# First stage traced in source order, the weight generator run in pairs, first weights requested on a second queue

## The chip, the core and the metric

The kernel runs on one core of a Trainium2 chip. The metric is the device time of one execution in microseconds (us); lower is better. A core has TensorE (PE: matrix products into PSUM, with a separate record, PEld, for loading the stationary operand), VectorE (DVE), ScalarE (ACT), GpSimd (POOL) and SyncE (SP, which here only issues DMAs). [...] The profile is one execution; its lines L12 are lines of the kernel before.

## What is computed

Four layers follow each other on x of 64 sequences, 64 tokens, 256 features, with a condition vector of 64 numbers for each sequence. The first layer, which the change is about, in the reference:

```python
scale = cond @ norm_w.T + 1.0
ms = jnp.mean(x * x, axis=-1, keepdims=True)
h = x * (scale[:, None, :] * jax.lax.rsqrt(ms + EPS))
u = h @ up_w.T                                  # up_w: 2048 x 256
val, gate = jnp.split(u, 2, axis=-1)
h = val * jax.nn.gelu(gate, approximate=False)
hq = act_quant(h)                               # round(h * 127 / max|h|), per token
wq = weight_quant(down_w)                       # -1, 0 or 1
y = hq @ wq.T + x
```

Then come attention with conditioned norms, a gated feed-forward layer with conditioned norms, a layer norm with a bias from the condition, and an adapter whose two matrices are made for every sequence from its condition (`(h_lang @ Wdd.T + bdd) * 0.1`: 64 x 32768 numbers for each of the two). This making of the adapter's matrices is the "generator" below.

## The kernel before, in words

**Stages.** The 4096 tokens are eight blocks (NBLK) of 512 (T), each of four tiles (TT) of 128. Stage one is layer one (`l0`) with the generator beside it, stage two attention with first parts of the feed-forward layer, stage three the rest. Between stages data goes through DRAM (`x1d`, `x2d`, and `s1d`, `s2d` for the generator's output).

**Exact products.** A product in full precision is `mm3` (L83, L84, L85): both operands are split in a high part (a cast to fp32r on ScalarE) and a low part (a subtraction on DVE or GpSimd), and three matmuls are summed.

**Stage one.** The loop at L380 runs over visits n = 0 to 33, one for each 128-token tile and two to drain. A visit calls `upper(n, 0)` and `upper(n, 1)`: each makes gate and value for half the hidden features, two banks of six matmuls of 512 columns (12 matmuls), then GELU on ScalarE (L336) and value times GELU on DVE (L337). Between the halves stands one generator unit: `gen_make` (four fp32 products of 64 x 64 by 64 x 512, eight matmul records, into two banks, L251), `gen_load` of a later unit's 512 KB (`gt`), and, after the second half, `gen_store` (two ScalarE copies to `stg`, L261, and two DMAs issued by GpSimd, L263). `quant(n)` (L343 to L349: maximum, scale, round, clip on DVE) ends in a transposing DMA on SP (`qt`), and `lower(n - 2)` multiplies `qt` with the ternary weights (L363, eight matmuls) and adds x (L364). Every fourth visit `prep` loads the next block twice (`xf` features first, `xt` tokens first), scales and splits it (L315, L198, L199) and finds the root mean squares (L191 on ScalarE, L182 and L184 on GpSimd).

**Things done once.** `cond_norm` (L113, L120) makes layer one's scale, `load_up(j)` loads and splits a quarter of the up weights (L280, L281), `ternary` and `ternary_rest` make the -1/0/1 weights (L291, L299, L304 to L306), `cond_rest` makes the other conditioning vectors (L113, L155, copies L143, L156). Hooks at chosen visits call `cond_rest` (visit 4), `weights` (the split of attention's weights, visits 8 to 15) and, in the last visits, attention's first steps: `a_start` (load, mean squares, scale L205), `a_norm` (transposes L212, L215, L216, split) and `a_ahead` (values, queries and keys).

**What sets the order.** In stage one and three a planner orders each engine's instructions by its own costs. In stage two, from L841 to L922, `manual_schedule` fixes the order of PE, ACT, DVE and POOL to that of the source. SP's DMAs are left to the planner in all stages. Buffers are handed out per tag; PSUM's eight banks all have one tag in stage one, the 512 KB blocks share five buffers (tag `x1`).

Of the kernel before, what the change touches and what calls it, by code (L numbers as in the profile page):

```python
# [36 lines left out]
def tile_kernel(ctx: ExitStack, tc, xT, x, condT, cw, upT, downT, qkvT, woT, ghT, outT_w,  # L37
# [52 lines left out]

    ident = const.tile([P, P], F32, name="ident")
# [4 lines left out]
    for s in range(2):  # L96
        nc.sync.dma_start(out=ct[s * 64:(s + 1) * 64], in_=condT)

    gl = pools["a"].tile([P, NB], F32, name="gl")
    nc.vector.tensor_scalar(gl, ct, 0.1, None, ALU.mult)  # L100
# [9 lines left out]
    def cond_vector(cwv):  # L110
        pb = bank("mm")
        for c in range(2):
            nc.tensor.matmul(pb[:, c * NB:(c + 1) * NB], lhsT=cwv[:, c * P:(c + 1) * P], rhs=ct[0:64],  # L113
                             start=True, stop=True)
        return pb[:, 0:2 * NB].rearrange("p (c b) -> p c b", c=2)

    def cond_norm():
        cwn = main.tile([64, D], F32, tag="st", bufs=2, name="cwn")
        nc.sync.dma_start(out=cwn, in_=cw[:, V_NORM, :])
        nc.vector.tensor_scalar(cv[:, V_NORM], cond_vector(cwn), 1.0, None, ALU.add)  # L120

    def cond_rest():
# [8 lines left out]
        nc.sync.dma_start(out=vc, in_=vecs)  # L131
        nc.vector.tensor_tensor(w2, vc[:, 1, :], vc[:, 1, :], ALU.mult)
        bo = main.tile([NB, D], F32, tag="junk", bufs=1, name="bo")
        nc.sync.dma_start(out=bo, in_=rows[0:1, :].broadcast_to([NB, D]))
        al = main.tile([NB, 3, D], F32, tag="xn", bufs=1, name="al")
        for v0 in (1, 5):
            n = min(4, 8 - v0)
            cwt = main.tile([64, 4, D], F32, tag="x1", bufs=X1, name=f"cwt{v0}")
            nc.sync.dma_start(out=cwt[:, :n], in_=cw[:, v0:v0 + n, :])
            for v in range(v0, v0 + n):  # L140
                src = cond_vector(cwt[:, v - v0])
                if v != V_LIN:
                    nc.vector.tensor_copy(cv[:, v], src)  # L143
                    continue

                th = main.tile([P, 2, NB], F32, tag="st", bufs=2, name="th")
                for c in range(2):
                    nc.scalar.activation(th[:, c], src[:, c], AF.Tanh, bias=vc[:, 3, c:c + 1])
                    nc.vector.tensor_scalar(th[:, c], th[:, c], vc[:, 2, c:c + 1], vc[:, 1, c:c + 1],
                                            ALU.add, ALU.mult)  # L150
                    nc.vector.tensor_scalar(cv[:, v, c], th[:, c], vc[:, 2, c:c + 1], None, ALU.add)
            for i, v in enumerate((V_AA, V_FA)):
                if v0 <= v < v0 + n:
                    pb = bank("mm")
                    nc.tensor.matmul(pb[:NB, :D], lhsT=ct[0:64], rhs=cwt[:, v - v0], start=True, stop=True)  # L155
                    nc.vector.tensor_copy(al[:, i], pb[:NB, :D])  # L156
        nc.vector.tensor_tensor(al[:, 2], al[:, 1], bo, ALU.mult)
        nc.gpsimd.dma_start(out=alphad.rearrange("v b d -> b v d"), in_=al)


    def split_steps(hi, lo, src, kc, n, step):
        v = src.rearrange("(c p) n -> p c n", p=P)
        for c in range(kc):
            for j in range(0, n, step):
                uid[0] += 1
                st = main.tile([P, 512], F32, tag="st", bufs=2, name=f"st{uid[0]}")
                nc.sync.dma_start(out=st[:, :step], in_=v[:, c, j:j + step])
                nc.scalar.copy(hi[:, c, j:j + step], st[:, :step])
                nc.vector.tensor_tensor(lo[:, c, j:j + step], st[:, :step],
                                        hi[:, c, j:j + step].bitcast(F32), ALU.subtract)  # L170
                yield True
# [63 lines left out]
    def gen_load():  # L235
        if gen_left:
            g, sd, k = gen_left.pop(0)
            ks = slice(k * 2 * GC, (k + 1) * 2 * GC)
            uid[0] += 1
            gt = pools["a"].tile([P, 2 * GC], F32, tag="gt", bufs=3, name=f"gt{uid[0]}")  # L240
            nc.sync.dma_start(out=gt, in_=g[:, ks])
            gen_loaded.append((gt, sd.rearrange("s b x y -> b s (x y)")[:, :, ks]))
# [23 lines left out]
    def l0(hooks):  # L266
# [8 lines left out]
        def load_up(j):  # L275
            js = slice(j * 512, (j + 1) * 512)
            st = main.tile([P, 2, 512], F32, tag="x1", bufs=X1, name=f"upst{j}")
            nc.sync.dma_start(out=st, in_=upT.rearrange("(c p) n -> p c n", p=P)[:, :, js])
            for c in range(2):
                nc.scalar.copy(up[0][:, c, js], st[:, c])  # L280
                nc.vector.tensor_tensor(up[1][:, c, js], st[:, c], up[0][:, c, js].bitcast(F32), ALU.subtract)  # L281

        def ternary():
            dv = downT.rearrange("(f p) d -> p f d", p=P)
            ones = main.tile([P, P], F32, tag="junk", bufs=1, name="ones")
            nc.gpsimd.memset(ones, 1.0)
            wd = [block(f"wd{j}") for j in range(2)]
            for j in range(2):
                nc.sync.dma_start(out=wd[j], in_=dv[:, 4 * j:4 * j + 4, :])
                wj = main.tile([P, 4, D], F32, tag="xn", bufs=1, name=f"wj{j}")  # L290
                nc.scalar.activation(wj, wd[j], AF.Abs, accum_out=sa[:, j:j + 1])  # L291
# [723 lines left out]
```

## Time and profile before

| what | us |
|---|---|
| median of three runs | 807.06 (805.04 to 807.66) |
| the profiled execution | 804.37 |
| its span, first to last instruction | 802.2 |
| TensorE busy in it | 763.5 |
| stage one's products, first to last `upper` | 11.3 to 266.6 |
| a steady visit of stage one | 7.70 |
| first scores of attention | 279.3 |

The span is what the profile sees of the execution; 2.2 us lie around it. "Busy" is the time in which an engine has an instruction running; matmuls overlap in their records, so steps from start to start tell more than durations. In the lines of waits, the number in brackets is the idle time ahead of an instruction and what ended it; "issue" is a wait for nothing that the profile shows. The granted clock is given as a share of TensorE's full speed.

### The profile page before, as it was taken

Reading aid. Unit: us, or ns where it says so; the run is one execution under the profiler, and the core shown is the slowest. Engines: PE = TensorE matmul, PEld = TensorE weight load, DVE = VectorE, ACT = ScalarE, POOL = GpSimd, SP = SyncE. Lnnn points to the kernel's source line nnn. Section 1 sums busy time; section 2 is a strip of 40 time slices with the busy share of each in tenths; the row PEclk is TensorE's granted clock in tenths of the full one; section 3 lists DMA queues with packets and bytes.
Section 4 is the critical chain, followed back from the end, with each engine's and each line's share of the span. In section 5 each row is a group of like instructions: output and inputs, shape, how many; then the busy total and the mean of one; then the engine's idle time right before and its main releaser. Section 6 shows DMA issues by size and latency. Waiting matters only on the chain.

```text
span 802.2 us, 17323 instructions
## 1 busy us (share of the span) xinstructions
PE 763.5 (95%) x7014; PEld 620.2 (77%) x7014; DVE 567.2 (71%) x935; ACT 370.5 (46%) x758; POOL 325.7 (41%) x300
## 2 busy tenths in 40 slices
PE   5999999999999979999999999879999999999996
PEld 3676766667667868888887878778888888888885
DVE  4885866667667679999989875555666666665755
ACT  6524542443443558887877673223233333333130
POOL 2212221222225315545545316945454545454500
PEclk9989999999999999999999999989999999999999
DMA  8997989878884764545655129616161616160401
GB/s 296 308 252 223 233 230 241 203 221 206 190 259 106 145 158 96 131 133 133 153 139 120 40 69 236 131 28 180 35 180 39 173 44 167 50 161 28 133 1 54
DMA packets 117135, 118.87 MB, mean 148 GB/s; under 512 B 39568, under 2 KB 100624, under 8 KB 117056
## 3 DMA queue, kind: packets, MB, share of 16 engines
q1 hardware_dynamic: 109568, 92.40, 46.1%
q0 software_dynamic: 7488, 25.37, 10.4%
q8 instruction: 55, 0.90, 0.5%
q14 instruction: 24, 0.20, 0.1%
HBM read 71.41 MB, written 29.56 MB: 126 GB/s over the span
## 4 chain that ended last, share of the span: by engine, by line
PE 79%; DVE 9%; issue 4%; POOL 3%; DMA 3%; ACT 1%; SPq 0%; DVEq 0%; POOLq 0%; ACTq 0%
PE mm L83 10%; PE mm L84 10%; PE mm L85 10%; PE gh L83 7%; PE gh L85 6%; PE gh L84 6%; PE mm L251 4%; PE acc L85 4%; PE mm L363 4%; PE acc L84 4%; PE acc L83 4%; DMA x2d<-ax 2%; PE mm L520 2%; PE mm L212 2%; PE mm L713 2%
## 5 line engine op out<-in xcount | busy, mean ns | idle before, releaser
L83 PE MATMUL mm<-up,xhl 128*128 128x512 f32 x256 | 108.9, 425 | 2.2 <-ACT up L280 2.2
L84 PE MATMUL mm<-up,xhl 128*128 128x512 f32 x256 | 102.8, 402 | 0.1
L85 PE MATMUL mm<-up,xll 128*128 128x512 f32 x256 | 102.5, 401 | 0.0
L83 PE MATMUL gh<-xhf,gh 128*128 128x512 f32 x244 | 99.2, 407 | 0.0
L84 PE MATMUL gh<-xlf,gh 128*128 128x512 f32 x244 | 95.6, 392 | 0.5 <-POOL xlf L199 0.5
L85 PE MATMUL gh<-xhf,gh 128*128 128x512 f32 x244 | 95.8, 393 | 0.0
L642 ACT CAST hhi<-sg 128x512 fp32r<-128x512 f32 x61 | 37.9, 621 | 119.1 <-DVE sg L623 119.1
L337 DVE SCALAR_TENSOR_TENSOR h<-mm,rs_l,g 128x512 f32<-128x512 f32 x64 | 47.7, 745 | 59.5 <-PE mm L85 36.5
L623 DVE TENSOR_TENSOR sg<-gh,sg 128x512 f32<-128x512 f32 x61 | 41.7, 683 | 64.8 <-PE gh L85 58.2
L85 PE MATMUL acc<-wout,hlo 128*128 128x256 f32 x256 | 74.0, 289 | 7.9 <-DVE hlo L643 7.9
L83 PEld LDWEIGHTS mm<-up,xhl 128*128 128x128 f32 x256 | 49.2, 192 | 38.5 <-issue 18.7
L336 ACT ACTIVATE g<-mm,rs_l 128x512 f32<-128x512 f32 x64 | 44.0, 687 | 73.0 <-PE mm L85 66.9
L83 PE MATMUL acc<-wout,hhi 128*128 128x256 f32 x256 | 73.4, 287 | 1.6 <-ACT hhi L642 1.6
L643 DVE TENSOR_TENSOR hlo<-sg,hhi 128x512 fp32r<-128x512 f32 x61 | 54.6, 895 | 26.7 <-ACT hhi L642 26.3
L84 PE MATMUL acc<-wout,hhi 128*128 128x256 f32 x256 | 73.3, 286 | 0.0
L216 POOL TENSOR_TENSOR xg<-xg,cv 128x512 f32<-128x512 f32 x32 | 33.2, 1046 | 70.7 <-DVE xg L215 70.7
L622 ACT ACTIVATE sg<-gh 128x512 f32<-128x512 f32 x61 | 36.3, 595 | 50.6 <-PE gh L85 50.6
L261 ACT COPY stg<-mm 128x512 f32<-128x512 f32 x64 | 35.3, 587 | 50.9 <-PE mm L251 50.9
L85 PEld LDWEIGHTS mm<-up,xll 128*128 128x128 f32 x256 | 49.0, 192 | 11.9
L84 PEld LDWEIGHTS mm<-up,xhl 128*128 128x128 f32 x256 | 49.3, 193 | 9.8 <-DVE up L281 0.6
L85 PEld LDWEIGHTS acc<-wout,hlo 128*128 128x128 f32 x256 | 49.5, 193 | 8.6 <-DVE hlo L643 8.6
L85 PEld LDWEIGHTS gh<-xhf,gh 128*128 128x128 f32 x244 | 46.0, 188 | 10.7
(189 smaller groups left out, 1905.7 us busy)
## 6 DMA issues: line engine op xcount, KB each, us to landing
gt<-in_g SPq DMA_DIRECT2D x32, 512.0 KB, 4.7
rows<-alphad SPq DMA_DIRECT2D x48, 256.0 KB, 4.0
s1d<-stg POOLq DMA_DIRECT2D x32, 256.0 KB, 5.1
s2d<-stg POOLq DMA_DIRECT2D x32, 256.0 KB, 4.8
vb<-vx SPq DMA_DIRECT2D x32, 256.0 KB, 4.5
wd<-s1d SPq DMA_DIRECT2D x32, 256.0 KB, 4.5
wu<-s2d SPq DMA_DIRECT2D x32, 256.0 KB, 5.6
xf<-in_xT SPq DMA_DIRECT2D x8, 512.0 KB, 7.0
```

Of the source, the lines that this page charges most:

```text
L83: nc.tensor.matmul(out, lhsT=l[0], rhs=r[0], start=first, stop=False)
L84: nc.tensor.matmul(out, lhsT=l[0], rhs=r[1], start=False, stop=False)
L85: nc.tensor.matmul(out, lhsT=l[1], rhs=r[0], start=False, stop=last)
L216: nc.gpsimd.tensor_tensor(b3(xg), b3(xg), bc(vb, c, i), ALU.add)
L251: nc.tensor.matmul(pb[s][c * 64:(c + 1) * 64], lhsT=gl[h], rhs=gt[h, c * GC:(c + 1) * GC], start=True, stop=True, tile_position=(64 * s, 6 ...
L261: nc.scalar.copy(stg[:, s], pb[s])
L336: nc.scalar.activation(g, pg, AF.Gelu, scale=rs[:, t:t + 1])
L337: nc.vector.scalar_tensor_tensor(h[:, ch * 512:(ch + 1) * 512], pv, rs[:, t:t + 1], g, ALU.mult, ALU.mult)
L622: nc.scalar.activation(sg, pg, AF.Silu)
L623: nc.vector.tensor_tensor(sg, pv, sg, ALU.mult)
L642: nc.scalar.copy(h_hi, sg)
L643: nc.vector.tensor_tensor(h_lo, sg, h_hi.bitcast(F32), ALU.subtract)
```

## The change

- `manual_schedule` is entered at the top, so stage one's PE, ACT, DVE and POOL follow the source too; its end stays where it was.
- The generator: in even visits from 2 on, two `gen_make` after each other between the halves, then two loads and two stores; odd visits have none. The first two units are made after the first two tiles' first products. `gt` has four buffers, not three.
- The up weights: `load_up` only loads, j = 2 and 0 on ScalarE's DMA queue as the first loads, j = 3 and 1 on SP after x and two generator blocks; `split_half` splits, the second half's subtraction on GpSimd. In the start the products of `upper(0, 0)` and `upper(1, 0)` are parted from the GELU. An early GELU on two columns (`sa`) stands ahead.
- `prep` is three steps in three visits (`prep_load`, `prep_parts`, `prep_scale`); `quant` rounds in place, before `lower` and, in the last visit, before the hooks; `lower(0)` moves to visit 3.
- `cond_rest` keeps its matmuls, but its loads go out in visit 3 (`cond_load`), its products go to three banks, and DVE copies several vectors at a time. `ternary`'s loads go to attention's memory, a visit earlier.
- Splitting of weights is a class `Splitter` that loads one piece ahead. Attention's first steps are spread over visits 25 to 33; the scale of block 2 (`a_scale(2)`) moves into attention's first step.

The diff, cut to its core:

```diff
+    ordered.enter_context(tc.manual_schedule(engines={mybir.EngineType.PE, mybir.EngineType.Activation, mybir.EngineType.DVE, mybir.EngineType.Pool}))
...
+        pbs = [bank("mm") for _ in range(3)]
         for v0 in (1, 5):
...
+            for v in range(v0, min(v0 + 4, 8)):
+                cond_vector(crest[v0][:, v - v0], pbs[v0 // 5], 2 * NB * (v - v0))
...
+        nc.vector.tensor_copy(cv[:, 1:5], src[0])
+        nc.vector.tensor_copy(cv[:, 5:7], src[1][:, 0:2])
+        nc.vector.tensor_copy(al[:, 0:2], pbs[2][:NB].rearrange("b (i d) -> b i d", i=2))
...
-            gt = pools["a"].tile([P, 2 * GC], F32, tag="gt", bufs=3, name=f"gt{uid[0]}")
+            gt = pools["a"].tile([P, 2 * GC], F32, tag="gt", bufs=4, name=f"gt{uid[0]}")
...
+        def split_half(j, c):
+            js = slice(j * 512, (j + 1) * 512)
+            st = ups[j]
+            nc.scalar.copy(up[0][:, c, js], st[:, c])
+            (nc.vector if c == 0 else nc.gpsimd).tensor_tensor(up[1][:, c, js], st[:, c],
+                                                              up[0][:, c, js].bitcast(F32), ALU.subtract)
...
+        load_up(2, nc.scalar)
+        load_up(0, nc.scalar)
+        prep_load(0)
+        nc.sync.dma_start(out=ct[64:128], in_=condT)
+        for _ in range(2):
+            gen_load()
+        load_up(3, nc.sync)
+        load_up(1, nc.sync)
...
+        nc.scalar.activation(sa, nhalf[:, 0:2], AF.Gelu)
...
         cond_norm()
+        split_half(2, 0)
+        for c, _ in enumerate(prep_parts(0)):
+            split_half((2, 0)[c], 1 - c)
+        split_half(0, 1)
+        prep_scale(0)
+        upper(0, 0, "products")
+        upper(1, 0, "products")
+        nc.vector.tensor_scalar(gl, ct, 0.1, None, ALU.mult)
+        gen_make()
+        gen_make()
+        for j in (3, 1):
+            for c in range(2):
+                split_half(j, c)
+        upper(0, 0, "rest")
+        upper(1, 0, "rest")
+        gen_store()
+        gen_store()
         gen_load()
...
         for n in range(N + 2):
             if n < N:
-                if n != 1:
+                if n > 1:
                     upper(n, 0)
+                if n % 2 == 0 and n > 0:
+                    gen_make()
+                    gen_make()
+                    gen_load()
+                    gen_load()
+                    gen_store()
+                    gen_store()
+                upper(n, 1)
...
+            if n < N - 1:
+                quant(n)
+            if n == 3:
+                lower(0)
+            if n >= 3:
                 lower(n - 2)
...
+    hooks = {3: [cond_load], 4: [cond_rest], 7: [splits.load]}
...
-    hooks[last - 5] = [lambda: a_start(0)]
-    hooks[last - 3] = [lambda: a_norm(0, 0), lambda: a_norm(0, 1)]
-    hooks[last - 2] = [lambda: a_start(1)]
+    hooks[last - 7] = [lambda: a_load(0)]
+    hooks[last - 6] = [lambda: a_begin(0)]
+    hooks[last - 5] = [lambda: a_scale(0), lambda: a_load(1)]
+    hooks[last - 4] = [lambda: a_norm(0, 0), lambda: a_begin(1)]
+    hooks[last - 3] = [lambda: a_norm(0, 1)]
+    hooks[last - 2] = [lambda: a_scale(1), lambda: a_load(2)]
...
-        if tp == 0 and w > 0:
+        if tp == 0:
             if i + 2 < NBLK:
                 a_scale(i + 2)
```

## The prediction, made before the changed kernel was run

> **What bounds the kernel now.** I read the page's busy shares first, then busy time by stretches, then the time line of TensorE in single visits.
>
> ```profile
> PE 763.5 (95%) x7014; PEld 620.2 (77%) x7014; DVE 567.2 (71%) x935; ACT 370.5 (46%) x758; POOL 325.7 (41%) x300
> ```
>
> TensorE carries the kernel. The change is in the first stage and its hand-over, so I cut that part of the span into stretches (us, then busy time per engine, granted clock, DMA share, GB/s):
>
> ```profile
> 0.00:11.31 11.31, 3.07 (x12) 1.26 (x12) 2.83 (x6) 3.48 (x6) 2.57 (x9) 1.00 0.68 227
> 11.31:28.21 16.90, 16.80 (x66) 11.40 (x67) 10.88 (x23) 14.18 (x30) 5.65 (x9) 1.00 1.04 381
> 63.80:266.56 202.76, 202.76 (x1057) 139.91 (x1053) 141.01 (x271) 86.13 (x188) 55.64 (x79) 1.00 0.82 212
> 266.56:279.32 12.76, 12.10 (x81) 10.16 (x80) 8.69 (x16) 7.91 (x21) 5.46 (x6) 1.00 0.72 138
> 279.32:296.17 16.85, 12.51 (x251) 10.91 (x252) 11.05 (x11) 9.08 (x16) 3.62 (x4) 0.93 0.78 189
> ```
>
> From 63.80 to 266.56 TensorE never pauses, so there only fewer or denser TensorE instructions count. Room lies before 11.31 (first up-projection product) and around the hand-over. A third place, inside "busy", is the conditioning step `cond_rest`:
>
> ```profile
> 51.35:56.58 5.23, 5.23 (x33) 3.90 (x32) 5.23 (x13) 0.52 (x2) 0.00 (x0) 0.85 1.09 238
> 56.58:58.05 1.47, 1.47 (x8) 1.04 (x8) 1.47 (x8) 0.00 (x0) 0.00 (x0) 0.50 1.06 376
> 58.05:61.86 3.81, 3.81 (x11) 3.04 (x10) 0.94 (x3) 0.79 (x2) 0.62 (x1) 0.50 1.34 202
> 61.86:69.55 7.69, 7.69 (x42) 5.27 (x41) 4.03 (x9) 4.15 (x14) 2.42 (x4) 1.00 0.63 191
> ```
>
> It takes 5.23 us, and the clock is halved within and after it.
>
> **Part 1: two generator units together.** One unit in a steady visit (start, duration):
>
> ```profile
> 124.06 0.40 PE L85 MATMUL mm<-up,xll 128*128 128x512 f32 x1
> 124.39 1.09 PE L251 MATMUL mm<-gt,gl 64*64 64x512 f32 x8
> 125.41 0.50 PE L83 MATMUL mm<-up,xhl 128*128 128x512 f32 x1
> 125.74 0.39 PE L84 MATMUL mm<-up,xhl 128*128 128x512 f32 x1
> ```
>
> Up products follow each other every 0.233 us. Into the unit the step is 0.33 (0.10 lost), the unit itself takes 1.02 from start to start, and out of it the step is 0.33 (0.10 lost): 1.22 us. The second four of its eight matmuls start at 124.86, 0.48 after the first four, and the change back costs 0.54. A unit directly behind another should pay two such steps, some 0.92, and no change of kind: 0.30 less. In the loop there are 15 pairs: **-4.5 us**. Bounds: 0 if the second unit waits for its banks, -6 at 0.41 saved. The four banks come back through four ScalarE copies of 0.59 us (L261), 2.4 us, in front of the next GELU. The copies overlap `upper(n, 1)` (2.8 us); with eight banks taken in turn TensorE asks for the pair's banks some 5 us after it ended. Hidden, except beside other ScalarE work: in visits 10 and 14, which have a norm (2.4 us) and a weight split as well, my tally of the queues leaves 0.53 each: **+1.1**.
>
> **Part 2: the start.** Before: the first generator block lands at 6.96, x at 8.26, the two up blocks at about 9.7 and 11.09; a 512 KB block every 1.36 us. After: ScalarE asks for the up blocks at about 0.7 and 1.2, SP for x as its third load at about 2.0. [...] Were it a path of its own, x would land 4.3 us after its issue (the first generator block's row), at 6.3. [...] three blocks at 1.36 after a first at about 5.0 make 7.5. The row of landings is one queue in strict turn[...]; I take 7.5. So the gain is the generator block that no longer goes ahead.
>
> From there: xs 0.64, the cast 0.60, first product at 8.9 (before 11.31). The low parts then pace it: five casts on ScalarE to 11.3, the last subtraction on GpSimd (1.3 us, row L199 on POOL) at 12.6, so `upper(0,0)` ends at 14.3. `upper(1,0)` follows. Before, products were 0.43 apart until 17.49, 6.2 us after the first one (the clock column has no record of this start and prints 1.00); I let the clock rise at 15.9, and `upper(1,0)` ends at 17.9. The pair 2.0, two more groups of products 5.6: `upper(2,0)` starts at 25.6. Before it starts at 28.21 with one generator unit (1.0) and L299 (0.35) more done: 26.9 for the same work. **-1.3 us**, between -3 (clock earlier) and +1 (weights j=3 and 1, now behind x and two generator blocks, late: due 19.9, landed by 14.5, split by 17.8). The second GELU table load (1.28) goes; ScalarE has the room, nothing.
>
> **Part 3: conditioning.** The loads (two `cwt`, `vc`, `bo`) go out a visit earlier, the same number on SP, whose order is not fixed by the source; DVE's eight small copies become three large. TensorE keeps its 28 L113 matmuls (0.12 apart) and four L155 (0.57 per pair at full clock): 3.4 + 1.1 = 4.5 instead of 5.2: **-0.7**. The half clock outside the step cost 0.67 in `lower` (1.47 against 0.80) and nine products at 0.43 instead of 0.233: 1.76; together **-2.4 if it does not recur**. [...] The rows decide: the clock fell at full "busy"[...]. [...] I take no drop, and keep 0 to -2.4.
>
> **Part 4: order of the source.** On DVE in-order queues cost: from the end of `upper(0,1)` (22.7) stand h 0.75, quant 3.0, h 0.75, the next block's parts 2.7, quant 3.0, two h 1.5, L297 0.16: 34.6. TensorE reaches L299 at 33.3 and waits 1.4 (with semaphores **+1.6**); behind it on its queue stands `upper(3,0)`. Then six ternary operations 4.2, two quants, four h: `lower(0)`'s last operation ends near 48.0, while `upper(4,1)` wants its bank at 47.2: **+0.75**. The 0.57 wait for wq at 38.40 goes: **-0.6**. In steady pairs DVE needs some 11.3 of 15.1: hidden. `quant` in place, `ones`, `wd` in other memory: nothing on a path.
>
> **Part 5: hand-over.** The 0.67 wait before the first scores goes, as both `lower` now follow the last copy: **-0.7**. But the norm scale of block 2 (L205, four, 1.13) moves into the first attention step, where DVE is back to back from 280.56 and TensorE already waits for it (0.93 at 287.21): **+1.1**. The load weights and x1 reads moved earlier sit under full TensorE.
>
> Sum: -4.5 + 1.1 - 1.3 - 0.7 - 2.4 + 1.6 + 0.75 - 0.6 - 0.7 + 1.1 = -5.6 us. Against the profiled execution (804.37, span 802.2) 798.8; that execution was 2.7 under the median of the runs, so for the median 807.06 - 5.6 = 801.4.
>
> **Rivals.**
> - *A stall elsewhere goes too.* Stages two and three hold gaps that nothing in this stage causes:
>
> ```profile
> 294.27 0.85 PE L539 MATMUL mm<-pts,vb 128*32 128x64 f32 x20 [3.38 <-issue]
> 525.70 0.58 PE L85 MATMUL acc<-wout,hlo 128*128 128x256 f32 x1 [7.67 <-DVE hlo L643]
> ```
>
> The first is between matmuls of one line, with data there, and an instruction packet is fetched at 291.54; its place can shift with the count of instructions ahead. The second comes from the planner's order in stage three, which the diff leaves alone. One gone: 3.4 or 7.7 more, 794 to 798. For it: they are accidents of place; against: nothing touches them, and new ones can appear.
> - *Nothing is left.* The clock drops all the same (+2.4), and x lands no earlier than before (+1.3): 805.1; with the second unit as dear as the first half of the time, 807.
> - *Slower: the transposed tile comes late.* In the visits that prepare a block, DVE now has h 0.75, parts 3.3 with the wait for the cast, quant 3.0 before the transpose goes out, 7.0 after the products; TensorE wants it after `lower` 0.8, a generator visit 8.6, two groups of products 5.7: 15.1. Slack 8.1 us; the landing is 4.3 in the median, 8.2 at most. From 8 us it decides. Behind a burst of two generator loads and four stores, 2 MB at 1.36 per 512 KB, it would be 4.3 + 5.4 = 9.7, 2 us late in seven visits: +13.5, so 815. Against it: DMA share 0.82, and the burst is spread over a visit.
>
> **Chances.** A move of less than 0.3% (2.4 us) can't be told from no change here. The forecast 0.50 (own range 798 to 805), the stall elsewhere 0.17, nothing left 0.18, the slower case 0.15. Of the first about 0.48 and of the third 0.03 lie under 804.6: faster 0.68, same 0.18, slower 0.14. The range 793 to 808 takes in the first three and leaves out the slow case and the ends.
>
> **What would show it.** Right: visits in pairs of 15.1 us, L251 x16 in one piece of about 1.95; first L83 near 8.9; no row at 0.50 clock after the conditioning step; waits of about 1.5 before L299 and 0.8 before `upper(4,1)`. Wrong: pairs at 15.4 or more; L363 waiting for qt; waits for the L261 copies; a first product after 10; a wait over 2 us before L520 in the first attention step.

## The result, and the profile after

The changed kernel takes 797.47 us in the median of four runs (794.82 to 799.51); the kernel before, run beside it, 806.94 (805.04 to 807.66). The ratio is 0.9888, with a 95% interval of 0.9858 to 0.9918: 9.5 us faster, where the prediction said 5.6. The profiled execution took 794.82 us with a span of 793.0, 9.2 less than the span of before. It is the fastest of the four and has the highest granted clock, 0.994 for 0.987 to 0.989 in the other three; what those lost, no profile shows. One of planner's twenty runs below, at 813.78 us, was in a slow state of the chip and is left out of its ratio.

First the page's row of TensorE, then busy time by stretches, cut as in the prediction (us from start to end, length; then busy time and count of TensorE, of its weight loads, of DVE, ScalarE and GpSimd; granted clock, DMA share, GB/s).

```profile
PE 752.4 (95%) x7014; PEld 618.7 (78%) x7014; DVE 575.8 (73%) x926; ACT 371.3 (47%) x758; POOL 326.2 (41%) x304
```

```profile
0.00:10.69 10.69, 1.09 (x5) 0.93 (x5) 2.12 (x5) 2.78 (x5) 2.62 (x9) 1.00 0.80 270
10.69:28.19 17.50, 17.02 (x65) 11.34 (x65) 9.98 (x13) 11.26 (x25) 9.53 (x10) 1.00 1.00 349
28.19:45.62 17.43, 15.59 (x84) 10.82 (x82) 16.25 (x29) 9.42 (x22) 4.00 (x6) 1.00 0.95 243
61.43:260.80 199.37, 199.37 (x1061) 142.43 (x1060) 154.63 (x282) 88.75 (x191) 52.26 (x79) 1.00 0.83 222
260.80:273.57 12.77, 12.10 (x82) 10.28 (x80) 6.93 (x14) 7.27 (x17) 4.54 (x4) 1.00 0.80 124
```

The row says where to look: TensorE executes the same 7014 matmuls and is busy 11.1 us less. The time went out of busy time (changes of kind, half clock), not out of idle time. Stretch by stretch: the first up product comes 0.6 us sooner (10.69 for 11.31), but the 16.90 us after it became 17.50, with the same two generator units in them. A third unit, which the kernel before made ahead of 11.31 while TensorE had nothing else to do, is now left for later; so the start got worse. The stretch from `upper(2,0)` to `upper(4,0)` has 1.84 us of idle TensorE (17.43 less 15.59), where before had 0.57. From 61.43 to 260.80 there is no idle time, as before. The hand-over is what it was, 12.77 for 12.76.

Now single visits on TensorE's time line (start, duration, engine, line, operation, output <- inputs, shapes). L269 of the changed kernel is L251 of before, the generator's matmul.

```profile
127.91 0.40 PE L85 MATMUL mm<-up,xll 128*128 128x512 f32 x1
128.24 1.95 PE L269 MATMUL mm<-gt,gl 64*64 64x512 f32 x16
130.12 0.50 PE L83 MATMUL mm<-up,xhl 128*128 128x512 f32 x1
130.46 0.39 PE L84 MATMUL mm<-up,xhl 128*128 128x512 f32 x1
```

From the product ahead of the pair (127.91) to the second one behind it (130.46) are 2.55 us; two ordinary steps of 0.233 off, the pair costs 2.08. The rows of before, read in the same way (124.06 to 125.74), give 1.21 for a unit and 2.43 for two: 0.34 less. Whole visits say the same. The first products of even visits, two in a row in the changed kernel, then two before:

```profile
80.09 0.48 PE L83 MATMUL mm<-up,xhl 128*128 128x512 f32 x1
95.15 0.48 PE L83 MATMUL mm<-up,xhl 128*128 128x512 f32 x1
```

```profile
82.91 0.48 PE L83 MATMUL mm<-up,xhl 128*128 128x512 f32 x1
98.31 0.48 PE L83 MATMUL mm<-up,xhl 128*128 128x512 f32 x1
```

They stand 15.06 us apart from 80.09 to 230.66 (150.57 for ten pairs), and 15.40 before (82.91 to 236.91). That is 0.34 a pair, 5.1 us for fifteen.

**Where the 9.2 us of the span lie.** The first scores start at 273.57 for 279.32: 5.75 us came from the first stage. The first product into `acc`, the end of the attention stage, is at 464.40 for 472.81: 2.7 us more came from a stage in which the change moves little. The last stage gave 0.8.

### The profile page after: what moved, and what is told of

The parts are those of the page before. It is cut to its first block, busy times and chain, and to the rows that moved or that the text cites. A ratio compares the mean times of both kernels' runs of the same rounds, so it can differ in the third digit from the quotient of the medians.

```text
span 793.0 us, 17333 instructions
## 1 busy us (share of the span) xinstructions
PE 752.4 (95%) x7014; PEld 618.7 (78%) x7014; DVE 575.8 (73%) x926; ACT 371.3 (47%) x758; POOL 326.2 (41%) x304
## 4 chain that ended last, share of the span: by engine, by line
PE 79%; DVE 8%; DMA 4%; issue 3%; POOL 3%; ACT 1%; SPq 1%; POOLq 0%; DVEq 0%; ACTq 0%
PE mm L83 10%; PE mm L85 10%; PE mm L84 10%; PE gh L83 6%; PE gh L85 6%; PE gh L84 6%; PE mm L269 4%; PE acc L85 4%; PE mm L396 4%; PE acc L84 3%; PE acc L83 3%; PE mm L587 2%; PE mm L230 2%; PE mm L606 2%; PE mm L794 2%
## 5 line engine op out<-in xcount | busy, mean ns | idle before, releaser
L83 PE MATMUL mm<-up,xhl 128*128 128x512 f32 x256 | 106.6, 416 | 2.2 <-ACT xhl L216 2.2
L84 PE MATMUL mm<-up,xhl 128*128 128x512 f32 x256 | 102.6, 401 | 0.5 <-DVE up L304 0.5
L83 PEld LDWEIGHTS acc<-wout,hhi 128*128 128x128 f32 x256 | 49.6, 194 | 4.2 <-ACT hhi L709 1.9
```

The lines of the kernel that those rows point to most:

```text
L83: nc.tensor.matmul(out, lhsT=l[0], rhs=r[0], start=first, stop=False)
L84: nc.tensor.matmul(out, lhsT=l[0], rhs=r[1], start=False, stop=False)
```

## The experiments

Each kernel was run beside the kernel before on the same chip, so ratios are compared, not times of different rows. Theory A was from the start: the paired units carry the gain and the other parts are small. Its rivals: the order of the source carries it; the second queue does; the packed conditioning step does.

| kernel | median us (runs) | ratio to before, 95% |
|---|---|---|
| after | 797.47 (4) | 0.9888 (0.9858 to 0.9918) |
| one_queue | 795.44 (4) | 0.9892 (0.9829 to 0.9955) |
| x_first | 799.69 (10) | 0.9926 (0.9899 to 0.9953) |
| one_unit | 803.55 (20) | 0.9987 (0.9966 to 1.0008) |
| old_cond | 816.04 (4) | 1.0135 (1.0078 to 1.0193) |
| planner | 806.35 (20) | 0.9996 (0.9973 to 1.0019) |
| cond_copies | 798.17 (4) | 0.9894 (0.9863 to 0.9925) |
| warm | 795.93 (4) | 0.9864 (0.9822 to 0.9906) |
| start | 794.16 (4) | 0.9844 (0.9808 to 0.9880) |
| tidy | 799.07 (6) | 0.9899 (0.9874 to 0.9925) |
| tidy_warm | 795.00 (6) | 0.9860 (0.9838 to 0.9882) |
| tidy_bufs | 800.00 (6) | 0.9914 (0.9893 to 0.9934) |
| start_warm | 792.50 (6) | 0.9833 (0.9797 to 0.9868) |

**one_unit: the pairs undone.**

```diff
-                if n % 2 == 0 and n > 0:
-                    gen_make()
-                    gen_make()
-                    gen_load()
-                    gen_load()
-                    gen_store()
-                    gen_store()
+                if n > 1:
+                    gen_make()
+                    gen_load()
+                    gen_store()
```

> The changed kernel with one generator unit in every visit instead of two in every other. Theory A (the pair saves one change between kinds of matmul, 0.34 us): visits of 7.70 us again, 15 times 0.34, so 5.1 us slower than the changed kernel (797.5): 802.6. Rival (source order and the moved copies make the visits shorter, the pairs do not matter): visits of 7.53, same time as the changed kernel.

803.55 us: with single units all the rest of the change is worth nothing that can be told from before (0.9987, the interval reaching over 1). Two visits take 15.40 us again, and the first scores come at 280.63, 7.06 after those of the changed kernel. Of these 5.1 are the pairs. The rest goes with a longer wait at the ternary product (2.22 for 1.35), a later clock at the start (full at 20.08 for 18.42) and a half clock of 3.41 us at 57.62; on the other side, the changed kernel's waits of 0.50 at `lower(1)` and 0.67 before the first scores are not there.

**planner: the order written by hand undone in the first stage**, with the pairs and all other edits kept.

```diff
-    ordered = ExitStack()
-    ordered.enter_context(tc.manual_schedule(engines={mybir.EngineType.PE, mybir.EngineType.Activation, mybir.EngineType.DVE, mybir.EngineType.Pool}))
 
     ident = const.tile([P, P], F32, name="ident")
...
+    ordered = ExitStack()
+    ordered.enter_context(tc.manual_schedule(engines={mybir.EngineType.PE, mybir.EngineType.Activation, mybir.EngineType.DVE, mybir.EngineType.Pool}))
     late = []
```

> The changed kernel with one thing undone: the hand-written order of TensorE, ScalarE, DVE and GpSimd begins again only at the attention stage, so the planner orders the first stage. Theory A (the gain is in the instructions themselves: fewer changes of kind of matmul, and an accidental gap in stage two): pairs of visits keep some 15.1 us, the wait before L322 (1.35) and the start change by 1 to 2 us either way, so within 3 us of the changed kernel, 795 to 801. Theory B (the order of the source carries the gain, because it keeps the two units together and the copies out of the way): the planner pulls the two units apart again or sets copies ahead of the GELUs, pairs go back to 15.4 and the first scores come 5 us later: 802 or more.

806.35 us, the time of before. Theory B has the size and not the reason: the pairs stay together (one x16 row of 1.95 us, as above), and without other waits a pair of visits takes 15.06. But `lower` waits for its transposed tile, in five visits: 1.70, 2.52, 1.77, 1.07 and 2.54, together 9.6 us. One of them on the time line (in square brackets the idle time before, and what ended it):

```profile
99.61 1.05 PE L394 MATMUL mm<-wq,qt 128*128 128x256 bf16 x8 [2.52 <-DMA qt<-q]
```

The tile that this one waited for was asked for at 91.69 and landed at 99.57, 7.9 us later. In the changed kernel the same tile was asked for at 83.54, right behind its products, and landed at 86.29; its `lower` runs at 94.34. So the planner's DVE is 8.2 us later with this tile, while its turn on TensorE came only 2.7 later (97.09), and the transposes are slower (median from issue to landing 4.71, longest 10.22; 3.40 and 8.90 in the changed kernel). This is the "slower" rival of the prediction, at 9.6 us where I had 13.5 (in an execution of 810.10, slower than planner's median). In the changed kernel only `lower(1)` waits so, 0.50; as far as these two profiles show, because the order of the source keeps DVE early. Beside one_unit it shows that the two parts need each other: order without pairs 0.9987, pairs without order 0.9996, both 0.9888.

**one_queue: the second queue undone.**

```diff
-        load_up(2, nc.scalar)
-        load_up(0, nc.scalar)
+        load_up(2, nc.sync)
+        load_up(0, nc.sync)
```

> The changed kernel with the first two blocks of up weights asked for on SP, behind ct and cwn and ahead of x, as in one queue. Theory A (the second queue lets 1 MB run ahead of the small condition weights): cwn lands near 4.4 us again (it landed at 7.2 in the changed kernel), x as third big block near 9, the first up product between 9.5 and 10.7, and the whole is 0 to 1 us faster than the changed kernel's 797.5. Theory B (a second queue is a path of its own): the up weights land 1.5 us later and the start loses 1 to 2 us.

795.44 us, ratio 0.9892 for 0.9888: the second queue is worth nothing that can be measured, though four runs leave an interval 10 us wide. The conditioning weights `cwn` land at 3.69 (for 7.23 in the changed kernel), the two up blocks at 6.38 and 7.95 (5.24 and 6.79), x at 9.28 (8.44); the first product starts at 10.77 for 10.69. What is won for one load is lost for another.

**x_first and start: what bounds the start.** x_first asks for x ahead of the two up blocks, on SP's queue; start does the same and, on ScalarE and DVE, sets x's scaling and parts ahead of the weights' casts:

```diff
-        split_half(2, 0)
-        for c, _ in enumerate(prep_parts(0)):
-            split_half((2, 0)[c], 1 - c)
-        split_half(0, 1)
+        for _ in prep_parts(0):
+            pass
+        for j in (2, 0):
+            for c in range(2):
+                split_half(j, c)
```

> The changed kernel with one queue and x ahead of the up weights: ct, cwn, x, two up blocks. Theory A (the start waits for cwn, then for x; the weights have time): cwn near 4.4, x near 6.5, first product near 8.5 instead of 10.7; the third tile's first product comes about 2 us earlier than 28.19, so 795.5 in all. Theory B (the weights pace the start): the first product is earlier, but the second weight block lands near 9 and the third tile's first product moves by less than 0.7 us.

> The changed kernel with x asked for ahead of the two up-projection blocks on SyncE, and on ScalarE and DVE x's scaling and parts ahead of the weights' casts and low parts (x alone first, with those left where they were, had gained nothing). Theory A (the start is bound by the order of landings and of the two engines' queues): x at 5.9, its parts done by 8.3, the first weights at 8.5, first product at 9.2 instead of 10.7, upper(0,0) no longer waits for low parts; upper(2,0) starts about 1.5 us sooner if the clock rises as long after the first product as in the changed kernel (6.8 us): 796. Theory B (all data of the start share the transfer rate, so that the last weight block sets it): first product near 10.5, nothing gained.

x_first missed what both theories expected. x landed at 5.90, and its first product still came at 11.14, because in the order of the source DVE has the weights' low part ahead of x's scaling, and ScalarE the weights' cast, which waits for an up block. The rows of DVE and ScalarE in x_first:

```profile
8.49 0.62 ACT L303 CAST up<-upst 128x512 fp32r<-128x512 f32 x1 [6.27 <-DMA upst<-in_upT]
9.14 0.69 DVE L304 TENSOR_TENSOR up<-upst,up 128x512 fp32r<-128x512 f32 x1 [3.92 <-ACT up L303]
9.75 1.29 DVE L346 TENSOR_TENSOR xs<-xf,cv 128x512 f32<-128x512 f32 x2
```

DVE stands idle 3.92 us in front of the low part, from 5.90 on with x there. In start the queue is turned round:

```profile
6.23 1.29 DVE L346 TENSOR_TENSOR xs<-xf,cv 128x512 f32<-128x512 f32 x2 [0.93 <-DMA xf<-in_xT]
...
9.08 0.79 PE L83 MATMUL mm<-up,xhl 128*128 128x512 f32 x1 [4.11 <-ACT up L303]
```

First product at 9.08, no wait for low parts behind it, `upper(2,0)` at 24.67 for 28.19; 794.16 us, ratio 0.9844. Theory A holds in kind; that start is faster than the changed kernel is shown by the rows, not by the times, whose intervals overlap. The 3.5 us at `upper(2,0)` are 1.6 of an earlier first product, 0.5 of the wait for a low part that went, and 1.4 of the clock: it was full 4.6 us after the first product here and 7.7 in the changed kernel, and each of the 3.1 us between loses 0.46 (steps of 0.43 for 0.233). What brought it up sooner is not shown. At `upper(8,0)` 1.9 are left, since a half clock of 3.41 us begins at 54.60.

**cond_copies and old_cond: the conditioning step.** cond_copies keeps the loads where the change put them and gives each vector a bank and a copy again, as before; old_cond puts the whole old step back, its loads too.

```diff
-        pbs = [bank("mm") for _ in range(3)]
         for v0 in (1, 5):
             for v in range(v0, min(v0 + 4, 8)):
-                cond_vector(crest[v0][:, v - v0], pbs[v0 // 5], 2 * NB * (v - v0))
...
+                one = cond_vector(crest[v0][:, v - v0], bank("mm"))
+                if v != V_LIN:
+                    nc.vector.tensor_copy(cv[:, v], one)
```

> The changed kernel with its early loads, but the conditioning step as before: a bank and a copy for each vector, eight small copies for three. Theory A (packing is worth only its own 0.8 us[...]): step of 5.2 instead of 4.44 us, with or without a half clock of 3.4 or 6.8 us behind it, 798 to 801 for 797.5. Theory B (packing is what keeps the clock up): a half clock of 6.8 us in or after the step that costs 2.4 us more, over 800.

> The changed kernel with the conditioning step of before: loads at visit 4, a bank and a copy for every vector. Theory A (its products are sparse for 5 us and halve the clock): 0.8 us more in the step and a row at half clock after it that costs another 2.4 to 3, in all 3 us or more slower: 800.5 to 802. Rival ([...]the packed form does not matter): under 1.5 us slower, no row at 0.50.

cond_copies: 798.17 us, ratio 0.9894: packing cannot be told from no packing. Its step takes 6.70 us from 52.86 to 59.56, with a wait of 0.61, for 4.27; a half clock of 6.83 us begins in it, at 55.67. old_cond is some 20 us slower than the changed kernel, far past both expectations, and for another reason than the one under test: TensorE waits for the conditioning weights themselves.

```profile
64.88 3.65 PE L116 MATMUL mm<-ct,cwt 64*128 64x64 f32 x16 [12.07 <-DMA cwt<-in_cw]
...
73.25 2.15 PE L116 MATMUL mm<-ct,cwt 64*128 64x64 f32 x9 [3.69 <-DMA cwt<-in_cw]
```

With a fixed order nothing can step ahead of these matmuls, and 23.89 us of half clock (from 55.88) go with the wait. The early loads, which I had costed at nothing, are what pays for the fixed order here.

**warm and start_warm: products to bring up the clock**, into a bank that nobody reads; warm has 30 in the changed kernel, start_warm 13 in start.

```diff
+    def warm(count):
+        pw = bank("mm")
+        for _ in range(count):
+            nc.tensor.matmul(pw[:, 0:P], lhsT=ident, rhs=ident, start=True, stop=True)
...
+        warm(5)
         cond_norm()
+        warm(8)
```

> The changed kernel with 30 fp32 products of the identity with itself (128x128, into a bank that nobody reads) put on TensorE ahead of the first up-projection, 22 ahead of the first conditioning product and 8 behind it. Theory A (the clock rises a fixed stretch of work after TensorE becomes busy): the clock is full at 10.7 when the first up product starts, products come 0.233 instead of 0.43 us apart, and the seven microseconds at half clock shrink to what DVE's and GpSimd's low parts allow: upper(2,0) starts 1.5 to 3 us before 28.19, the end likewise. Theory B (the start is paced by the low parts, and the clock only looks like the limit): upper(2,0) within 0.5 us of 28.19. The count of TensorE instructions ahead of stage two shifts by 60: if the gaps that are put down to issue hang on the place in the instruction stream, they move to other matmuls.

> The kernel called start with 13 fp32 products of the identity with itself, 5 ahead of the first conditioning product and 8 behind it, into a bank that nobody reads; at half clock each took 0.43 us in the run called tidy_warm, so that they fill TensorE from 1.35 to about 8.6 and no longer hold up the first up product (there 30 of them had put it off to 13.1). Theory A (the clock rises 3.3 to 9.1 us after TensorE begins to be busy, the spread of the runs so far, so that starting 7.7 us sooner takes away most of the 4.6 us of half clock in start): 1 to 2 us less than start, ratio 0.982 to 0.983. Theory B (at full clock the low parts pace the first products, and the wait brings the half clock back): the ratio of start, 0.984, or up to 0.986.

In warm the clock is full at 4.61, but `upper(2,0)` starts at 28.23, where it did: theory B for the start. TensorE runs out of low parts, and the clock is taken back for 3.41 us at 14.85:

```profile
12.78 0.50 PE L84 MATMUL mm<-up,xhl 128*128 128x512 f32 x1 [0.35 <-POOL up L310]
...
15.02 0.79 PE L84 MATMUL mm<-up,xhl 128*128 128x512 f32 x1 [0.96 <-DVE up L310]
```

start_warm is the fastest kernel of the study: 792.50 us, ratio 0.9833 (0.9797 to 0.9868), 13 us less than before. Against start (0.9844) the intervals overlap, so the products' own worth isn't shown by the times. `upper(2,0)` is only 0.6 sooner (24.05). The larger difference lies in the attention stage: waits there that the profile puts down to "issue" are 0.52 us in all, for 3.56 in start. The same in the other two kernels with added products: 0 in warm (4.85 in the changed kernel) and 0 in tidy_warm (4.51 in tidy). The eleven kernels without added products have 1.14 (planner) to 6.36 us (before) of them, mostly at the same matmuls block after block (358, 382, 406 and 430 us in the changed kernel; 357, 382, 406, 430 in one_queue), with sizes that differ. Beside them stand the packets of a DMA queue that the page lists, 16 KB each:

```profile
q8 instruction: 55, 0.90, 0.5%
```

Each of the 52 waits of this kind in the attention stage, over all profiles, ends 1.2 to 1.7 us after such a packet has landed (at 404.35 for the changed kernel's wait that ends at 405.84). That TensorE waits there for its next instructions is my reading; no run tries it by itself, and why the added products take nearly all of these waits away stays open.

**tidy, tidy_warm and tidy_bufs: the waits that were left.** tidy is start with the ternary sum a visit earlier, and with block 2's scaling between the first stage and the first scores:

```diff
                 nc.scalar.activation(wj, til["wd"][j], AF.Abs, accum_out=sa[:, j:j + 1])
+            nc.vector.tensor_tensor(sb[:, 0:1], sa[:, 0:1], sa[:, 1:2], ALU.add)
...
-            nc.vector.tensor_tensor(sb[:, 0:1], sa[:, 0:1], sa[:, 1:2], ALU.add)
...
+    a_scale(2)
     late = []
...
-        if tp == 0:
+        if tp == 0 and w > 0:
```

> The kernel of the run called start (x asked for first, its parts ahead of the weights' casts, one queue) with two more edits. The sum of the two ternary row sums is put on DVE a visit earlier, ahead of the next block's parts, instead of behind two further products; and the scaling of block 2 is done between the first stage's last tile and the first scores, where DVE waits anyway, instead of inside the first attention step. Theory A (both waits are only late DVE instructions): the 1.4 us before the ternary product and some 0.4 to 0.8 of the 1.3 us in the first attention step go, 1.5 to 2 us in all: 792 to 793. Theory B (a wait taken away in front of full TensorE work comes back at the next late thing, here the transposed tile that lower(1) waits 0.5 us for): no more than 0.5 us gained, 794.

> The kernel called tidy with 30 fp32 products of the identity with itself ahead of the first up product, 10 ahead of the first conditioning product and 20 behind it, into a bank that nobody reads. Theory A (the clock rises 3 to 4 us after TensorE begins to be busy, and what follows runs at full clock as long as it is fed): the 4.3 us of half clock after the first product (9.1 to 13.4) go, 1.5 to 2 us: 790.5 to 791.5. Theory B (at full clock TensorE runs out of low parts, waits a microsecond as it did at 15.0 in the run called warm, and the clock is taken back): within 1 us of tidy.

> The kernel called tidy with two buffers instead of four for the adapter's weights of the last stage, down and up, so that the planner can no longer bring the next block's four wide bias additions ahead of the normalization's inverse root on GpSimd. It bears on the 7.8 us wait of TensorE near 515, which the change left as it was. Theory A (the wait is those four additions, 9.4 us on GpSimd's queue): the wait and the half clock in it, 3.4 to 6.8 us, go: 7.8 plus 1.5 to 3 us less, some 782 to 785. Theory B (the inverse root is late for another reason, or the planner puts other work in that place; weights that are loaded later come late themselves): less than 3 us gained, or slower.

799.07 us: tidy is slower than start by the medians (the ends of the intervals still overlap). The ternary wait of 1.40 is gone, and `lower(1)` waits 2.25 for its transposed tile instead of 0.49:

```profile
40.95 1.05 PE L398 MATMUL mm<-wq,qt 128*128 128x256 bf16 x8 [2.25 <-DMA qt<-q]
```

The scaling does worse. I had read DVE as free there; it is, but the scale factor isn't ready:

```profile
273.44 1.38 DVE L223 TENSOR_SCALAR xna<-ax,rs_a 128x256 f32<-128x256 f32 x4 [2.31 <-POOL rs_a L202]
274.74 1.21 DVE L558 TENSOR_REDUCE mx<-S 128x16 f32<-128x1024 f32 x1
```

DVE waits 2.31 us for GpSimd's inverse root, with the maximum of the first scores queued behind it; the first attention step takes 11.79 us instead of 10.39. Two half clocks of 3.41 us at 319.98 and 347.28 come on top; start's profile has none there, so not all of the loss need be these two edits. By the rows, the change has this scaling at the better place. tidy_warm (30 products) is 4.1 us below tidy, but not at the start: its first product comes at 13.11, since TensorE was busy from 1.35 and still got the full clock only at 10.48, so that the products and the conditioning step between them filled 11.8 us. The attention stage is what is shorter: 192.0 us from the first scores to the first product into `acc`, for 196.7. tidy_bufs (two buffers for four, for the adapter's weights) was to take away the 7.8 us in the last stage, which start and the changed kernel share:

```profile
517.20 0.58 PE L85 MATMUL acc<-wout,hlo 128*128 128x256 f32 x1 [7.81 <-DVE hlo L710]
```

The four additions did go from in front of the inverse root, and TensorE waits 6.72 and 2.09 us all the same. Theory A fell; the rows of tidy_bufs name another guest in the queue:

```profile
515.50 0.42 ACT L209 ACTIVATE junkf<-fx 128x256 f32<-128x256 f32 x1 [13.21 <-DMA fx<-x2d]
```

```profile
517.72 0.19 POOL L200 TENSOR_SCALAR ms_f<-ssf 128x4 f32<-128x4 f32 x1 [9.33 <-ACT junkf L209]
517.99 1.02 POOL L202 TENSOR_TENSOR rs_ln<-ms_ln,nhalf 128x4 f32<-128x4 f32 x1
```

ScalarE waits for the load of a later block (`fx` from `x2d`) that the planner put ahead of the next cast; GpSimd waits for that in front of the finished block's inverse root. What the load waits for stays open.

## Why the prediction was right, point by point

The time is inside the range, and the pairs, its largest term, are right in kind. But 797.47 lies just under the 798 to 805 of the forecast's own case, in the 794 to 798 of its first rival; and up to the first scores the sum came out by errors that cancelled, which is luck. The terms one by one:

**The pairs** (-4.5, 0.30 each): right in kind and nearly in size, 0.34 each and 5.1 us. The second unit begins 0.91 after the first, as I had it (0.92). One_unit shows that they carry the gain; planner that they give nothing where the order lets the transposed tiles be late.

**The bank waits of visits 10 and 14** (+1.1): not there. From 61.43 to 260.80 TensorE has no idle time at all. My tally set the four copies of the pair in front of one GELU, beside the norm's work; the cover of 5 us was enough.

**The start** (-1.3): the step that failed. For equal work `upper(2,0)` stands at 28.19 where 26.9 would have been level: 1.3 us later, not sooner. It stood 2.6 us later than the 25.6 I had. Three terms were missed. The first, 1.8 us, is the first product, in these rows of the changed kernel, first TensorE, then DVE and ScalarE:

```profile
7.37 1.08 PE L116 MATMUL mm<-ct,cwn 64*128 64x64 f32 x4 [7.37 <-DMA cwn<-in_cw]
...
8.70 0.68 DVE L304 TENSOR_TENSOR up<-upst,up 128x512 fp32r<-128x512 f32 x1
9.29 1.29 DVE L344 TENSOR_TENSOR xs<-xf,cv 128x512 f32<-128x512 f32 x2
10.02 0.62 ACT L216 CAST xhl<-xs 128x512 fp32r<-128x512 f32 x1 [4.14 <-DVE xs L344]
```

I followed x and the up blocks to their landings and forgot the third load, the conditioning weights `cwn`. It is 64 KB, issued at 1.36, and landed at 7.23 behind two blocks of 512 KB on the other queue (4.35 before, 3.69 in one_queue). `cv` waits for it, x's scaling for `cv`, and by then the low part of the weights stands ahead of it on DVE (8.70 to 9.29). So 10.69 instead of 8.9. Of these 1.8 us about half is the low part in front of x's scaling, for which x had to wait from 8.44 to 9.29; the other half is x itself, 8.44 for 7.5 (my own figures, a first block at 5.0 and two more at 1.36 each, make 7.7). That the second queue would not be a path of its own was my estimate, and it held: x landed at 8.44, not at 6.3, and one_queue takes the same time (0.9892 for 0.9888). But I had followed that to x alone, and the small load paid. The second term is the low parts behind the first product: `upper(0,0)` took 6.4 us, with a wait of 0.48 and longer steps, where I had 5.4; that costs some 0.5 (an estimate: what takes 1.0 us in steps of 0.43 takes 0.54 in steps of 0.233). The third is the clock: I let it rise 7.0 us after the first product and it took 7.7, which from 10.69 is 18.42; some 0.3.

**The conditioning step** (-0.7): 4.27 us for 5.23, -1.0.

```profile
53.47 3.33 PE L116 MATMUL mm<-ct,cwt 64*128 64x64 f32 x28
56.73 1.07 PE L151 MATMUL mm<-cwt,ct 64*64 64x256 f32 x4
57.74 1.05 PE L396 MATMUL mm<-wq,qt 128*128 128x256 bf16 x8
```

**The half clock** (-2.4 if it doesn't recur): it doesn't in the profiled run, where 53.20 to 57.80 has a clock of 1.00. But of the eleven kernels with the packed step and the early loads only this one and tidy_warm are free of it: it lasts 3.41 us in one_queue, one_unit, start, tidy and tidy_bufs, and 6.83 in x_first, planner, warm and start_warm, as it does without packing (before and cond_copies, 6.83). So packing shortens it at best. I had counted a chance as an effect; the profile that the sum was to meet happened to have it. That I took no drop for the likeliest was my estimate, which no run stood behind; the runs have none in two kernels of the eleven.

**The ternary wait** (+1.6): 1.35. **The wait of `upper(4,1)` for a bank** (+0.75): not there; in its place `lower(1)` waits 0.50 for its transposed tile. **The wait for wq** (-0.6): gone, -0.57. tidy shows that these are one chain: DVE late with the second visits' work, and what is taken from one wait goes to the next.

**The hand-over** (-0.7): nothing. The 0.67 before the first scores is there again.

```profile
273.57 1.20 PE L546 MATMUL S<-kb,qf 32*64 32x128 f32 x64 [0.67 <-DVE x L397]
```

Before, it was put down to ScalarE's copy of the queries (`qf`, L457), which ended at 279.26; DVE's last tile had ended only 0.09 us earlier. The change brought the copy forward and left the tile, so the wait stayed. In one_unit, warm and start_warm the scores follow the last `lower` without this wait; what decides that isn't shown.

**The moved scaling** (+1.1): the first attention step has two waits, 0.78 and 0.52, for one of 0.93: +0.4. The whole step, from the first scores to the second, takes 10.39 us for 9.57, +0.8; so the size was nearly right.

The measured terms to the first scores, with the half clock at my 2.4: -5.1 + 1.3 - 1.0 - 2.4 + 1.35 + 0.5 - 0.57 = -5.9, and the trace has -5.75. The prediction's terms to that point make -6.75. So up to there the sum was right by errors of both signs: the start was 2.6 us too good, three waits too dear by 1.6 in all, the pairs and the conditioning step too small by 0.9, the hand-over too good by 0.7.

**What made 9.5 out of 5.6.** Behind the first scores the span lost another 3.5 us where I had 1.1 more. Most of that is the first rival, *a stall elsewhere goes too*: the wait of 3.38 us put down to issue at 294.27, with a half clock of 3.41 us beside it, is 0.47 in the changed kernel.

```profile
286.44 0.52 PE L606 MATMUL mm<-pts,vb 128*32 128x64 f32 x18 [0.47 <-issue]
```

The first two attention steps, which hold it, take 21.47 us for 24.97. (Other waits of the kind grew: in the whole stage they went from 6.36 to 4.85 us.) But the changed kernel issues as many TensorE instructions ahead of them as before, so my reason ("its place can shift with the count of instructions ahead") doesn't cover this run: the wait stands at the same place, the first weighing of values, and its size differs (0.33 to 1.85 in one_queue, x_first, start and tidy). In the kernel before, the packet of instructions at 291.54 set out 0.65 us after TensorE had run dry at 290.89; in the other 51 waits it set out 0.9 to 2.7 us ahead of that. Why it was late this once stays open; each kernel has one profile. The other stall of that rival, 7.67 at 525.70, stayed (7.81). Of the rival *nothing is left* the half about the start came true, and the half about the clock in nine of eleven kernels; the pairs outweighed them.

## What to carry to other kernels

Before costing a load that goes out sooner, list all loads that the first instruction waits for, small ones above all, and follow the one that lands last through its engine's queue; here a load of 64 KB behind two of 512 KB on another queue held up the work on x (putting it first alone gained no time, since x then landed later). A fixed order of the source pays when every load and every slow copy is early enough to be there: here it was worth nearly 9 us with early loads (0.9888 for 0.9996), and with the conditioning loads left late the kernel was 11 us slower than before (1.0135). Where a gain comes from fewer changes of kind on the bound engine, count it from visits at steady state; where it is a half clock that might not recur, keep it out of the likeliest sum and in the range.

## What the runs showed of the hardware that was not expected

- The clock came up 3.1 to 9.3 us after the first dense product in kernels without added products (planner 3.1, one_queue 3.7, tidy 4.0, start 4.6, after 7.7, x_first 8.0, one_unit 9.3), and 3.3, 7.7 and 9.1 us after TensorE began to be busy in warm, start_warm and tidy_warm. No fixed delay fits these times, and what sets them is not shown. Three stretches of the changed kernel, the last one from 18.42 on, where its clock is up, with seven, nine and 22 matmuls; the profile has no record of a lower clock ahead of 18.42 and prints 1.00 (the steps of 0.43 us from product to product, then 0.233, show it):

```profile
11.60:15.01 3.41, 2.93 (x7) 1.37 (x7) 3.18 (x3) 3.31 (x12) 2.55 (x3) 1.00 1.04 392
15.01:18.42 3.41, 3.41 (x9) 2.63 (x10) 2.79 (x3) 2.39 (x5) 3.33 (x4) 1.00 1.04 381
18.42:21.83 3.41, 3.41 (x22) 2.02 (x24) 0.95 (x2) 0.77 (x2) 0.69 (x1) 1.00 1.08 363
```

  In the first of them TensorE waits 0.48 us for a low part. In one_queue the clock was up at 14.45, just ahead of the same wait (0.48 us, to 14.93); in start, which has no such wait, at 13.7. Whether the wait bears on the clock, no run tries by itself.
- The clock fell while TensorE's records leave no gap: in the kernel before, TensorE was busy for all of the 5.23 us of the conditioning step (51.35 to 56.58), with a clock of 0.85 in the mean and 0.50 behind it. A half clock of 3.41 or 6.83 us begins within or just behind that step's small products (64 rows, 64 columns) in eleven of the fourteen profiles; the changed kernel and tidy_warm have none there. What decides it is not shown. One_queue, then the changed kernel (the clock is the third number from the end):

```profile
52.00:55.41 3.41, 3.41 (x28) 2.92 (x27) 1.81 (x8) 0.31 (x2) 0.00 (x0) 1.00 1.16 52
55.41:58.82 3.41, 3.41 (x13) 2.50 (x13) 3.00 (x7) 0.21 (x2) 0.64 (x1) 0.50 0.90 234
```

```profile
52.56:55.97 3.41, 3.41 (x27) 2.95 (x26) 1.72 (x7) 0.31 (x1) 1.13 (x3) 1.00 1.11 336
55.97:59.38 3.41, 3.41 (x24) 2.58 (x24) 2.11 (x6) 0.52 (x2) 0.10 (x1) 1.00 0.79 282
```

- In the three kernels with 13 to 30 products added at the start, nearly all waits put down to issue are gone from the attention stage, 270 us later (0, 0 and 0.52 for 4.85, 4.51 and 3.56, and 1.14 to 6.36 in all kernels without them); why is not shown. All 52 in the fourteen profiles end 1.2 to 1.7 us after a packet of instructions has landed.
